# Four fused layers on one core: the first sequence's picked rows fetched as 32x32 tiles and turned by VectorE, and a new order of VectorE's work in the linear and the gated attention

## The chip, the core and the metric

The kernel runs on one core of one Trainium2 chip. A core has five engines with an instruction queue each: TensorE (PE in the profile; its weight loads are listed apart as PEld), VectorE (DVE), ScalarE (ACT), GpSimd (POOL) and SyncE (SP), which here issues nearly all transfers between the chip's memory (DRAM) and the core's working memory (SBUF). Matmuls write into eight accumulator banks (PSUM). The metric is the device time of one execution in microseconds (us), as a median of several runs.

## The reference

Two sequences of 1024 rows with 512 columns go through four layers. Each adds its result to its input and normalises every row.

```python
x = layernorm(x + linear_attention(x))     # 16 heads of 32
x = layernorm(x + fp4_ffn(x))              # 512 -> 2 x 1408 -> 512
x = layernorm(x + gated_attention(x))      # 16 heads, chunks of 64 rows
x = layernorm(x + expert_ffn(x))           # 512 of 1024 rows per sequence

# linear attention
q = elu(x @ Wq.T) + 1;  k = elu(x @ Wk.T) + 1;  v = x @ Wv.T
kv = einsum('bhtd,bhte->bhde', k, v)
z  = 1 / (einsum('bhtd,bhd->bht', q, k.sum(rows)) + 1e-6)
out = einsum('bhtd,bhde,bht->bhte', q, kv, z) @ Wo.T

# FP4 feed-forward: weights unpacked from 4-bit codes, one scale per 128 inputs
y = (silu(x @ w_gate.T) * (x @ w_up.T)) @ w_down.T
y = y / sqrt(mean(y * y) + 1e-6)

# gated attention
q = softmax(x @ Wq.T);  k = sigmoid(x @ Wk.T);  v = x
gf = log_sigmoid(-k)                 # decay, summed within a chunk of 64
o  = chunked_scan(q, k, v, gf)       # state S is carried from chunk to chunk
go = o @ Wog.T + x @ Wig.T
out = (o * rsqrt(mean(o * o) + 1e-5) * g_norm_w * silu(go)) @ Wo.T

# expert choice: the 512 rows with the highest score of each sequence
scores = x @ router_weight + router_bias
top, indices = top_k(scores, 512)
h = gelu(x[indices] @ w1 + b1)
out = zeros.at[indices].add((h @ w2 + b2) * sigmoid(top))
```

[...]

## The kernel before

The 2048 rows are held in SBUF in four blocks of 512 (two per sequence), `x_t[blk]`, each as four groups of 128 rows. Engines run their own queues in order; the order in a queue comes from a scheduler that follows the order of the program, and `tc.issue_after(ins)` tells it to place what follows behind a given instruction of the program. That is a hint of order, not a wait of its own. The feed-forward layer is ordered by hand.

**Seven products.** The large products (`by_seven`, `o_products`, `gate`, `hidden`) use a scheme with seven half-size products in place of eight: sums of input quarters are made first, products accumulate in a bank called `grow` and in side banks (`P2`, `P7`), and VectorE adds the results into place. A product's banks come from rings of banks (`rings["mm"]`, `rings["acc"]`), so a product can start only when VectorE or ScalarE has read what the bank held before.

**Linear attention** (lines 500 to 745). For each sequence b with blocks i = 2b and j = 2b + 1, the function `run(products, *others)` goes through the steps of one block's seven products and puts other work between them: `some_xk` (k times x, line 442), `turns` (PE turns weighed q rows, tile `qTp`, line 235), `some_o` (steps of `o_products`, the output products, whose results VectorE adds to x on line 571), `weigh` (lines 483 to 489: VectorE multiplies q with the sum of k, reduces it, takes the reciprocal and scales q), and `job(n)` (n steps of unpacking FP4 weights: a read of the packed codes `pk`, two VectorE steps on lines 288 and 289, one ScalarE step on line 292; `pk` has two buffers). In line 467 (`ksumb`) PE spreads the sum of k, which POOL adds up on lines 459 and 461. When a block's `o_products` are through, their last step takes the rows' statistics on VectorE (lines 226, 227, 218) and normalises the block on POOL: one power (line 219), four scalings of 128x512 (line 221). `split_quarter` (lines 264 to 268) turns the first block's rows for the next layer and splits them into a high part (ScalarE) and a low part `x1Tl` (VectorE, line 268).

**FP4 feed-forward** (lines 750 to 1300). Chunks of the hidden size pass through `gatep`, `upp` and `yp` products. `Normed.product` (line 1000) scales one row group's `yp` bank right after its product. At the end of the last chunk four groups are scaled; then the gated layer's first decayed keys follow (line 845, tile `rw`) and PE's first state updates (`up`, line 855).

**Gated attention** (loop over blocks from line 1875). `gate(blk)` is a generator: products `go`, with lines 1430 and 1431 multiplying a result into `uT`, later lines 1446 and 1449. `finish_by_seven` or `finish` (line 1515, tile `ao`) projects the result. Block 0 and block 1 are normalised for the router by `scored_rows` (line 221, and the score on line 1533, four each). `route` ranks the rows, and an indirect transfer by POOL (line 1579) scatters the picked rows into the DRAM table `picked`.

**Expert feed-forward.** `fetch` reads the picked rows back and turns them:

```python
nc.sync.dma_start(out=xs, in_=picked[b].rearrange("(c p) d -> p c d", p=P)[:, :, :C])
for i in range(4):
    pt = transposed(xs[:, i], "xsTp")
    nc.scalar.copy(room[:, :, i * P : (i + 1) * P], pt.rearrange("p (k t) -> p k t", k=KC))
```

`sums_of_x` (VectorE) makes their sums, `sums_of_w1` (VectorE, line 1980) those of the weights, `hidden` (line 1642, tile `hp`) multiplies them. `unpicked(blk)` takes statistics, normalises a block and writes it out (`out<-x`, line 1600), so that the rows that weren't picked have their result.

Of the kernel before, what the change touches and what calls it, by code (L numbers as in the profile page):

```python
# [21 lines left out]
P = 128  # L22
B, T, C = 2, 1024, 512
NB = 4
# [49 lines left out]
def body(ctx: ExitStack, tc: tile.TileContext, a: dict, out: bass.AP):  # L74
# [139 lines left out]
    def layernorm(x, mv, eps=1e-5, by=nc.vector):  # L214

        n = x.shape[1]
        rs = sp.tile([P, 4], F32, tag="rs", name="rs")
        nc.vector.tensor_scalar_add(rs[:, :n], mv[:, :, 1], eps)  # L218
        power = nc.gpsimd.tensor_tensor(rs[:, :n], rs[:, :n], const("mhalf")[:, :n], ALU.pow).ins  # L219
        for i in range(n):  # L220
            by.tensor_scalar(x[:, i], x[:, i], mv[:, i, 0:1], rs[:, i : i + 1], ALU.subtract, ALU.mult)  # L221
        return power
# [41 lines left out]
    def split_quarter(parts, blk, i, room=mm_bank):  # L264
# [3 lines left out]
        nc.vector.tensor_sub(lo, pt, hi.bitcast(F32))  # L268
# [111 lines left out]
    def by_seven(x, w, T, rooms, pairs, ready):  # L380
# [27 lines left out]
        nc.vector.tensor_add(c11, c11, p2)  # L408
# [69 lines left out]
    def weigh(blk, t):  # L478

        for r in range(2):  # L480
            x = pairs_of["q", blk][t][:, r]
            e = wk.tile([P, C], F32, tag="e", name="qk")
            nc.vector.tensor_mul(e, x, ksum_of[blk // 2])
            z = sp.tile([P, 16], F32, tag="z", name="z", bufs=2)
            nc.vector.tensor_reduce(z, e.rearrange("p (h d) -> p h d", d=32), AX.X, ALU.add)
            nc.vector.tensor_scalar_add(z, z, 1e-6)
            nc.vector.reciprocal(z, z)
            x3 = x.rearrange("p (h d) -> p h d", d=32)
            weighed[0] = nc.vector.tensor_mul(x3, x3, z.unsqueeze(2).to_broadcast([P, 16, 32])).ins

    weighed = [None]
# [61 lines left out]
    def o_products(blk):  # L553
# [6 lines left out]
        def product(ps, a, b, first, t, o):  # L560
# [10 lines left out]
            return nc.vector.tensor_add(x, x, ps.rearrange("p (r c) -> p r c", r=2)).ins  # L571
# [25 lines left out]
        yield  # L597
        mv = mv_of[blk] = sp.tile([P, 4, 2], F32, tag="mv", name="mv")
        with tc.issue_after(weighed[0]):
# [3 lines left out]
        yield  # L603
# [79 lines left out]
    def q_products(blk, ready):  # L683
        return by_seven(xT[blk], Wq, Ts["q"], S_rooms, pairs_of.setdefault(("q", blk), []), ready)
# [6 lines left out]
    for b in range(B):  # L691
        i, j = 2 * b, 2 * b + 1
        if b:
            run(
                k_products(i),
                turns(1, 0, 1) + job(1), job(1),
                turns(1, 2, 3) + some_o(1, 1) + job(1), some_o(1, 2) + job(1), some_o(1, 5) + job(1),
# [3 lines left out]
            k_products(j), [],  # L701
            some_xk(i, 0, 1) + job(2), some_xk(i, 2) + job(1) + q_ready, some_xk(i, 3) + job(1), job(1 + b),
# [3 lines left out]
        else:  # L706
# [7 lines left out]
            q_products(i, lambda t: weigh(i, t)), [],  # L714
            some_xk(j, 0, 1) + job(1 + b), some_xk(j, 2) + step(spread_ksum, b) + job(1), some_xk(j, 3) + job(1 + b),
        )
        if b == 0:
# [4 lines left out]
            q_products(j, lambda t: None),  # L722
# [4 lines left out]
            step(all_free) + some_o(i, 1) + step(weigh, j, 0) + split[3] + some_o(i, 3) + step(weigh, j, 1) + some_o(i, 1)  # L727
            + job(1 - b),
# [193 lines left out]
    with tc.tile_pool(name="s2", bufs=1) as wk2:  # L922
# [58 lines left out]
        class Normed:  # L981
# [8 lines left out]
            def product(self, i, g):  # L990
# [7 lines left out]
                if g == NI - 1 and i == 0:  # L998
                    self.y = place_w(3, "y")
                nc.vector.tensor_tensor(self.y[:, i] if g == NI - 1 else ps, ps, ratio[:, g], ALU.mult)  # L1000
# [174 lines left out]
        with tc.manual_schedule(engines={mybir.EngineType.PE, ACT, DVE, POOL}):  # L1175
# [38 lines left out]
            y_pair(LAST - 1, 1)  # L1214
            two = chunk_banks[1 - LAST % 2]
            free_banks = iter([*two, y_banks[3]])
            next_bank = lambda name: bank_tile(next(free_banks), name)
            gates.decayed(gates_at[3], gates_at[3], next_bank)
            new_spare(2)
            front(0, gates, gR["T2"][:, :, :P], next_bank)  # L1220
# [5 lines left out]
        rings["mm"] = (*chunk_banks[1 - LAST % 2], *y_banks[:2])  # L1226
        rings["acc"] = (*chunk_banks[LAST % 2], *y_banks[2:])
# [295 lines left out]
    def scored_rows(blk, mv=None):  # L1523

        if mv is None:
            mv = sp.tile([P, 4, 2], F32, tag="mv", name="mv")
            for i in range(4):
                row_stats(mv[:, i], x_t[blk][:, i])
        layernorm(x_t[blk], mv)
# [543 lines left out]
```

## Time and profile before

| What | us |
|---|---|
| Median of 3 runs | 896.24 (895.79 to 896.49) |
| The profiled execution's own time | 895.37 |
| Its span | 893.6 |
| PE busy within the span | 879.2 (98%) |
| DVE busy | 686.7 (77%) |
| ACT busy | 379.0 (42%) |
| POOL busy | 261.3 (29%) |

The granted TensorE clock is 0.997 over the span. Busy shares are an average over four layers with different limits. All times below are measured from the span's start. In the feed-forward layer, from 240 to 480 us, PE is busy 239.82 of 240 us; DVE is busy 49.08 of the 50 us from 85 to 135, and 57.76 of the 66 us from 605 to 671.

A line of the trace's time views gives the start, the time to the end of the last instruction of a group, the engine, the line of the program, the operation and its tiles, the number of instructions, and in brackets the idle time of that engine before it with what ended that idle time. In the list of waits the three numbers are the sum, the count and the longest.

### The profile page before, as it was taken

The numbers are of one execution on the slowest core, as the hardware profiler recorded it, in microseconds if no ns is written. First come the engines' busy times: TensorE is split into PE (matmuls) and PEld (weight loads), VectorE is DVE, ScalarE is ACT, GpSimd is POOL, SyncE is SP. The second block draws the span as 40 slices with busy tenths as digits, with TensorE's granted clock in tenths as the row PEclk, the third lists the DMA queues.
The fourth block names the chain that finished last, engine by engine and source line by source line (L and its number), as shares of the span: only waits on it lengthen the run. The fifth ranks groups of instructions, "written<-read, shape, count | busy, mean of one in ns | idle before, by whom it ended". The sixth has DMA issues, their size and how long they took to land. (4 is left out here: it accounts for less than half of the span.)

```text
span 893.6 us, 10909 instructions
## 1 busy us (share of the span) xinstructions
PE 879.2 (98%) x3923; PEld 687.5 (77%) x3923; DVE 686.7 (77%) x1320; ACT 379.0 (42%) x648; POOL 261.3 (29%) x229
## 2 busy tenths in 40 slices
PE   9999999999999999999999999999999999999996
PEld 6668876688678888888876787788586888888886
DVE  3569995589787787887779986848976976998535
ACT  2345342463477797887867333221202223210000
POOL 2020075200474358556655320020340030000112
PEclk9999999999999999999999999999999999999998
DMA  9632221211421503414102344000034220320001
GB/s 327 222 98 80 73 68 48 74 45 19 97 110 48 47 1 86 57 55 111 25 25 73 69 114 169 1 1 1 6 106 141 78 95 1 133 104 1 12 36 48
DMA packets 88007, 64.85 MB, mean 73 GB/s; under 512 B 63214, under 2 KB 63770, under 8 KB 87441
## 3 DMA queue, kind: packets, MB, share of 16 engines
q1 hardware_dynamic: 85313, 58.89, 22.9%
q0 software_dynamic: 1920, 4.22, 1.2%
q10 hardware_dynamic: 720, 1.05, 0.4%
q8 instruction: 31, 0.51, 0.2%
q14 instruction: 23, 0.19, 0.1%
HBM read 48.37 MB, written 17.88 MB: 74 GB/s over the span
## 5 line engine op out<-in xcount | busy, mean ns | idle before, releaser
L1000 DVE TENSOR_TENSOR yp<-yp,ratio 128x512 f32<-128x512 f32 x160 | 103.3, 693 | 17.2 <-PE yp L941 16.7
L219 POOL TENSOR_TENSOR rs<-rs,table 128x4 f32<-128x4 f32 (+1 forms) x19 | 17.2, 906 | 299.2 <-DVE rs L218 298.9
L966 ACT ACTIVATE gatep<-gatep,scale 128x512 f32<-128x512 f32 x132 | 83.9, 659 | 35.8 <-PE gatep L941 26.5
L941 PE MATMUL gatep<-x1Th,wgu 128*128 128x512 f32 x176 | 70.2, 399 | 0.0
L941 PE MATMUL yp<-wdn,hhi 128*128 128x512 f32 x176 | 70.1, 398 | 0.0
L941 PE MATMUL yp<-wdn,hlo 128*128 128x512 f32 x176 | 69.9, 397 | 0.2 <-POOL hlo L975 0.2
L941 PE MATMUL gatep<-x1Tl,wgu 128*128 128x512 f32 x176 | 69.3, 394 | 0.3 <-DVE x1Tl L268 0.3
L941 PE MATMUL upp<-x1Tl,wgu 128*128 128x512 f32 x176 | 68.8, 391 | 0.0
L941 PE MATMUL upp<-x1Th,wgu 128*128 128x512 f32 x176 | 68.8, 391 | 0.0
L966 ACT ACTIVATE upp<-upp,scale 128x512 f32<-128x512 f32 x100 | 64.9, 664 | 6.7 <-PE upp L941 3.7
L975 POOL TENSOR_TENSOR hlo<-whole,hhi 128x512 fp32r<-128x512 f32 x43 | 55.6, 1292 | 3.5
L974 POOL CAST hhi<-whole 128x512 fp32r<-128x512 f32 x43 | 26.3, 612 | 88.4 <-DVE whole L972 86.9
L972 DVE SCALAR_TENSOR_TENSOR whole<-upp,scale,silu 128x512 f32<-128x512 f32 x43 | 32.3, 750 | 19.8 <-PE upp L941 11.5
L909 PE MATMUL go<-spare,spare 128*128 128x256 f32 x192 | 44.5, 382 | 0.0
L442 PE MATMUL xk<-pair,x 128*128 128x512 f32 x96 | 42.7, 592 | 0.0
L226 DVE BATCH_NORM_STATS2 st<-x 128x6 f32<-128x512 f32 x64 | 42.3, 678 | 0.4
L909 PEld LDWEIGHTS go<-spare,spare 128*128 128x128 f32 x192 | 35.8, 190 | 7.4 <-issue 2.8
L941 PEld LDWEIGHTS yp<-wdn,hhi 128*128 128x128 f32 x176 | 33.1, 188 | 9.5 <-DVE yp L1000 1.0
L941 PEld LDWEIGHTS gatep<-x1Th,wgu 128*128 128x128 f32 x176 | 33.0, 188 | 9.2 <-ACT gatep L966 1.1
L941 PEld LDWEIGHTS gatep<-x1Tl,wgu 128*128 128x128 f32 x176 | 33.1, 188 | 8.2 <-DVE x1Tl L268 0.6
L941 PEld LDWEIGHTS yp<-wdn,hlo 128*128 128x128 f32 x176 | 33.1, 188 | 8.0 <-POOL hlo L975 0.6
L941 PEld LDWEIGHTS upp<-x1Th,wgu 128*128 128x128 f32 x176 | 33.1, 188 | 7.3 <-DVE rw L972 0.2
(469 smaller groups left out, 2067.8 us busy)
## 6 DMA issues: line engine op xcount, KB each, us to landing
pk<-in_gu SPq DMA_DIRECT2D x16, 352.0 KB, 3.7
x<-in_x SPq DMA_DIRECT2D x4, 1024.0 KB, 14.9
w<-in_w SPq DMA_DIRECT2D x1, 4096.0 KB, 12.3
xs<-picked SPq DMA_DIRECT2D x4, 1024.0 KB, 4.9
out<-x SPq DMA_DIRECT2D x4, 1024.0 KB, 4.5
w<-in_w SPq DMA_DIRECT2D x4, 1024.0 KB, 7.4
x0T<-in_xT SPq DMA_DIRECT2D x3, 1024.0 KB, 7.3
x1r<-x SPq DMA_DIRECT2D x3, 1024.0 KB, 5.1
```

The lines of the kernel that those rows point to most:

```text
L219: power = nc.gpsimd.tensor_tensor(rs[:, :n], rs[:, :n], const("mhalf")[:, :n], ALU.pow).ins
L226: nc.vector.bn_stats(st, x)
L442: ins = nc.tensor.matmul(acc_of[b][c], x_t[blk][:, i, c * P : (c + 1) * P], pairs_of["k", blk][i // 2][:, i % 2], start=blk % 2 == 0 and i ...
L909: ins = nc.tensor.matmul(ps[:, 256 * m : 256 * m + 256], w[:, k, m], b[:, k, 256 * half : 256 * half + 256], start=first and m == 0 and k ...
L941: nc.tensor.matmul(ps, w, x, start=start and n == 0, stop=stop and n == 1, skip_group_check=True)
L966: nc.scalar.activation(ps, ps, AF.Copy, scale=s)
L972: nc.vector.scalar_tensor_tensor(self.whole, ps, s, self.silu, ALU.mult, ALU.mult)
L974: nc.gpsimd.tensor_copy(hi, self.whole)
L975: nc.gpsimd.tensor_sub(lo, self.whole, hi.bitcast(F32))
L1000: nc.vector.tensor_tensor(self.y[:, i] if g == NI - 1 else ps, ps, ratio[:, g], ALU.mult)
```

## The change

Four places change.

1. **Linear attention.** The statistics and the normalisation leave `o_products` and become `norm(blk)`. In the second sequence's schedule block 0 is normalised within the k products of block 3, block 1 within the q products of block 2, and block 2 at the very end behind the weighing of block 3. Several VectorE steps are ordered behind others: the weighing of odd blocks behind additions of the output products, the `x1Tl` subtractions and one addition of `by_seven` behind the weighing. PE's turning of rows for block 1 moves behind the second product (`P<-Wk`). Unpacking steps are distributed differently, 27 in all as before.
2. **End of the FP4 feed-forward.** For the last two row groups of the last chunk the scaling is parted from the product: products, then the decayed keys, then the scalings. The banks that the first state updates use, and the two rings behind them, are exchanged accordingly.
3. **Gated attention.** `scored_rows` and `unpicked` are parted into statistics with the root (`root_of_rows`), which stay where they were, and the scaling with what follows it, which moves behind steps of the gate. Both treat the rows of block 0: they are scored in block 1's turn of the loop, now behind that turn's last gate addition, and normalised for the output in block 3's turn, now behind line 1431. The sums of w1 are ordered behind that line too.
4. **First sequence's picked rows.** One read of 1 MB, 16 PE transposes and 4 ScalarE copies are replaced by 16 reads of 64 KB (32 partitions, each 16 runs of 128 bytes) and 4 VectorE transposes of 32x32 tiles over 128x512. The reads are issued by SP when block 3's turn in the loop begins. The second sequence's `fetch` is as before.

```diff
+    def root(mv, eps=1e-5):
...
         nc.vector.tensor_scalar_add(rs[:, :n], mv[:, :, 1], eps)
+        nc.gpsimd.tensor_tensor(rs[:, :n], rs[:, :n], const("mhalf")[:, :n], ALU.pow)
+        return mv, rs
+
+    def to_norm(x, mv, rs, by=nc.vector):
+        for i in range(x.shape[1]):
             by.tensor_scalar(x[:, i], x[:, i], mv[:, i, 0:1], rs[:, i : i + 1], ALU.subtract, ALU.mult)
...
         nc.scalar.copy(hi, pt)
-        nc.vector.tensor_sub(lo, pt, hi.bitcast(F32))
+        with tc.issue_after(weighed[0]):
+            nc.vector.tensor_sub(lo, pt, hi.bitcast(F32))
...
         p2 = product(mm_bank("P2"), A12, B21, True)
-        nc.vector.tensor_add(c11, c11, p2)
+        with tc.issue_after(behind_add) if behind_add else contextlib.nullcontext():
+            nc.vector.tensor_add(c11, c11, p2)
...
+            with tc.issue_after(adds[-2 + r]) if blk % 2 else contextlib.nullcontext():
+                nc.vector.tensor_mul(e, x, ksum_of[blk // 2])
...
-            return nc.vector.tensor_add(x, x, ps.rearrange("p (r c) -> p r c", r=2)).ins
+            adds.append(nc.vector.tensor_add(x, x, ps.rearrange("p (r c) -> p r c", r=2)).ins)
+            return adds[-1]
...
+    def norm(blk):
+
         mv = mv_of[blk] = sp.tile([P, 4, 2], F32, tag="mv", name="mv")
-        with tc.issue_after(weighed[0]):
+        with tc.issue_after(anchor[0] if blk < 2 else weighed[0]):
             for i in range(4):
                 row_stats(mv[:, i], x_t[blk][:, i])
             layernorm(x_t[blk], mv, by=nc.gpsimd)
-        yield
...
-                turns(1, 0, 1) + job(1), job(1),
-                turns(1, 2, 3) + some_o(1, 1) + job(1), some_o(1, 2) + job(1), some_o(1, 5) + job(1),
+                [], turns(1, 0, 1),
+                turns(1, 2, 3) + some_o(1, 1), some_o(1, 2), some_o(1, 4) + [lambda: anchor.__setitem__(0, adds[-1])] + job(1),
...
-            k_products(j), [],
-            some_xk(i, 0, 1) + job(2), some_xk(i, 2) + job(1) + q_ready, some_xk(i, 3) + job(1), job(1 + b),
+            k_products(j), job(b),
+            some_xk(i, 0, 1) + job(2), some_xk(i, 2) + job(1 + b) + q_ready,
+            some_xk(i, 3) + (step(norm, 0) if b else []) + job(1 + b), job(1 + b),
...
-            q_products(i, lambda t: weigh(i, t)), [],
-            some_xk(j, 0, 1) + job(1 + b), some_xk(j, 2) + step(spread_ksum, b) + job(1), some_xk(j, 3) + job(1 + b),
+            q_products(i, lambda t: weigh(i, t)), job(b),
+            some_xk(j, 0, 1) + (step(norm, 1) if b else []) + job(1 + b), some_xk(j, 2) + step(spread_ksum, b) + job(1), some_xk(j, 3) + job(1 + b),
...
-            step(all_free) + some_o(i, 1) + step(weigh, j, 0) + split[3] + some_o(i, 3) + step(weigh, j, 1) + some_o(i, 1)
-            + job(1 - b),
+            step(all_free) + some_o(i, 1) + split[3] + some_o(i, 1) + step(weigh, j, 0) + some_o(i, 2) + step(weigh, j, 1)
+            + (step(norm, i) if b else []) + job(1 - b),
...
+                if scaled:
+                    self.scale(i, g)
+
+            def scale(self, i, g):
+
+                ps = self.ps[i]
                 nc.vector.tensor_tensor(self.y[:, i] if g == NI - 1 else ps, ps, ratio[:, g], ALU.mult)
...
-            y_pair(LAST - 1, 1)
+            for i in (2, 3):
+                normed[NB - 1].product(i, NI - 1, False)
             two = chunk_banks[1 - LAST % 2]
-            free_banks = iter([*two, y_banks[3]])
+            free_banks = iter([*two, y_banks[1]])
             next_bank = lambda name: bank_tile(next(free_banks), name)
             gates.decayed(gates_at[3], gates_at[3], next_bank)
             new_spare(2)
+            for i in (2, 3):
+                normed[NB - 1].scale(i, NI - 1)
             front(0, gates, gR["T2"][:, :, :P], next_bank)
...
-        rings["mm"] = (*chunk_banks[1 - LAST % 2], *y_banks[:2])
-        rings["acc"] = (*chunk_banks[LAST % 2], *y_banks[2:])
+        rings["mm"] = (*chunk_banks[1 - LAST % 2], y_banks[0], y_banks[3])
+        rings["acc"] = (*chunk_banks[LAST % 2], y_banks[2], y_banks[1])
...
+    def scored_rows(blk, mv=None, rooted=None):
+
+        to_norm(x_t[blk], *(rooted or (root(mv) if mv is not None else root_of_rows(blk))))
...
+    def unpicked(blk, rooted=None):
+
+        to_norm(x_t[blk], *(rooted or root_of_rows(blk, 0.25e-5)))
...
             with tc.issue_after(scored_next):
-                scored_rows(0)
+                rooted = root_of_rows(0)
...
         if blk == 3:
+            xsS = xT_tile("xs")
+            for g in range(4):
+                for k in range(KC):
+                    at = P * k + 32 * g
+                    nc.sync.dma_start(
+                        out=xsS[32 * g : 32 * g + 32, k].rearrange("j (tr i) -> j tr i", i=32),
+                        in_=picked[0][:, at : at + 32].rearrange("(tr j) i -> j tr i", j=32),
+                    )
             with tc.issue_after(scored):
-                unpicked(0)
+                rooted = root_of_rows(0, 0.25e-5)
...
+            if n == 3 and blk == 1:
+                with tc.issue_after(done):
+                    scored_rows(0, None, rooted)
+            if n == 1 and blk == 3:
+                with tc.issue_after(done):
+                    unpicked(0, rooted)
+                p7_added = done
...
-    sums_of_w1((0,))
-    _, xs = fetch(0)
+    xs = xT_tile("xsT")
+    with tc.issue_after(p7_added):
+        sums_of_w1((0,))
+        for i in range(4):
+            nc.vector.transpose(xs[:, :, tile_of(i)], xsS[:, :, tile_of(i)])
     xs = sums_of_x(xs, W1oT)
     finish(3)
-    sums_of_w1((1,))
+    with tc.issue_after(p7_added):
+        sums_of_w1((1,))
```

## The prediction

> **What bounds the kernel now.** I read the busy times first, then the waits of PE, then the chain, then the time views of VectorE, POOL and SP around each wait.
>
> ```profile
> span 893.6 us, 10909 instructions
> PE 879.2 (98%) x3923; PEld 687.5 (77%) x3923; DVE 686.7 (77%) x1320; ACT 379.0 (42%) x648; POOL 261.3 (29%) x229
> ```
>
> PE is idle for 893.6 − 879.2 = 14.4 us, of which the start takes 1.04 and the tail behind PE's last product (886.25) 7.35. So the change can win only PE work that it takes away and what is left of PE's waits.
>
> ```profile
> PE go L909 <- DVE uT L1431: 2.2, 2, 1.9
> PE grow L565 <- DVE x L571: 1.5, 2, 0.8
> PE up L855 <- DVE rw L845: 0.8, 1, 0.8
> PE grow L565 <- DVE qS L520: 0.6, 1, 0.6
> PE P L565 <- DVE x L571: 0.4, 1, 0.4
> PE gatep L941 <- DVE x1Tl L268: 0.3, 1, 0.3
> ```
>
> Each of these ends with a VectorE instruction in a stretch where VectorE is full (49.08 of 50 us busy from 85 to 135, 57.76 of 66 from 605 to 671). PE waits because of the order of VectorE's queue. The chain shows the PE work in question:
>
> ```profile
> 670.67 3.72 PE go L909 x16
> 674.39 1.75 PE xsTp L235 x16
> 676.13 13.74 PE ao L1515 x32
> 689.87 10.36 PE hp L1642 x48
> ```
>
> PE's own queue loses those 16 transposes and otherwise only changes places. So a wait that goes moves everything behind it forward, as long as nothing else comes late.
>
> **1. Linear attention.** Waits of 0.40 (99.85), 0.68 (102.53), 0.55 (118.91) and 0.82 (130.36). The first two: x<-P on line 571 starts at 99.12, because line 347 ahead of it waits for ScalarE's `e` until 98.51; its product was done at 97.73. Now it stands ahead of lines 483 and 485, so it runs at 97.75 and x<-grow near 99.7: both waits go. The turning of block 1's rows now stands behind `P<-Wk` (near 106.7), and the weighed rows end at 103.5 and 105.6, so no new wait there. The third and fourth are late VectorE queues, with eight statistics and POOL's normalisation in the same stretch:
>
> ```profile
> 115.97 10.41 POOL L221 TENSOR_SCALAR x<-x,mv,rs 128x512 f32<-128x512 f32 x4
> 228.45 8.26 POOL L221 TENSOR_SCALAR x<-x,mv,rs 128x512 f32<-128x512 f32 x4
> ```
>
> Beside the first, line 519 took 1.09, line 288 1.01 and line 347 1.75 us, against 0.5 to 0.69 elsewhere. With statistics and normalisation gone, line 520 is ready near 113.8 (PE wants it at 117.3) and line 571 reads near 126 (PE 127.9). Gain 0.40 + 0.68 + 0.55 + 0.82 = 2.45.
>
> Where it goes: VectorE is busy 12.98 of 26 us from 135 to 161 and 16.09 of 25 from 161 to 186, so its time there costs nothing. POOL is the question. Block 1's normalisation now stands ahead of the last four sums of k, which `ksumb` waits for. Before, these sums ended at 165.0 and PE read them at 175.21; after, PE reads at 175.21 − 2.45 = 172.76. The statistics end near 155.9 (the last pair's elu at 152.2, then 3.5 us of statistics and a `pk` step). Then one power (1.01 to 2.04), four scalings (8.26 to 10.54) and four sums (2.62 + 2.78 = 5.4; 5.1 to 5.7) end between 170.5 and 174.4: 2.2 us early to 1.6 late. The nearest execution of the same scalings stands at 138.95, with a power of 1.05 and 10.54; that gives 155.9 + 1.05 + 10.54 + 5.4 = 172.9, and I take 0.2 as lost.
>
> The Trainium skill, "SBUF — State Buffer", section "SBUF: two separate sides", says that VectorE and GpSimd lock a shared port pair for a whole instruction and the other blocks fully. The trace bears it out in part: VectorE's steps did grow beside the scalings, but the scalings took 10.41 us beside a full VectorE (10.40 of 10.40 busy), 10.54 beside one that was half idle (5.39 of 10.6), and 8.26 beside another (4.95 of 8.4). By the rule a VectorE busy 16.09 of 25 us leaves POOL between these, below 10.4, and the 0.2 falls away; by the nearest row it stays. The unpacking steps (27 as before) only move. Their reads land in 3.7 us on two buffers, and the longest wait of VectorE for one was 3.29 (145.29), in the half idle stretch. In front of the k products of the next pair VectorE has 1.8 us left; a read 1.8 us later than that would cost.
>
> End of the layer: the fourth `x1Tl` is ready near 211.0 for 215, so 0.30 (216.64) goes. Weighing block 3 moves later: its first half is ready at 216.13 for PE's 216.17, its second at 218.18 for 217.52. I take 0.5 lost (0 to 0.7). Block 2's normalisation (POOL until 236.71) is used by transfers needed at 256.3, 20 us of cover. Sum of the part: 2.45 + 0.30 − 0.2 − 0.5 = 2.05.
>
> **2. End of the FP4 layer.** `up` waits 0.75 for line 845 at 489.48, which stands behind four scalings (487.09, 2.48). With two of them behind it, its input (ScalarE, 487.80) decides and it ends near 488.7; PE's transposes before `up` end near 489.1. Gain 0.75, with about 0.4 us in hand. The two delayed scalings move the normalisation's inputs by 1.2 us; VectorE is continuous from 494.7 to 512, but at 494.70 it waits 1.49 us for PE, which absorbs them.
>
> **3. Gated attention.** Waits of 0.25 (574.07) and 1.91 (670.67), both for line 1431.
>
> ```profile
> 664.64 0.16 DVE L218 TENSOR_SCALAR rs<-mv 128x4 f32<-128x4 f32 x1
> ...
> 666.30 1.92 DVE L221 TENSOR_SCALAR x<-x,mv,rs 128x512 f32<-128x512 f32 x4 [0.90 <-POOL rs L219]
> ...
> 669.93 0.68 DVE L1431 TENSOR_TENSOR uT<-uT,go 128x512 f32<-128x512 f32 x1
> ```
>
> Here line 1431 stands behind a normalisation that waits for POOL's power, and a sum of w1. With them behind it, it runs when its product is there: about 570.4 in block 1's turn, 662.2 to 662.8 in block 3's, where the `go` products run through to 669.0. Both waits go: 2.16. Moved behind: in block 1's turn 1.82 + 4 × 0.61 = 4.28 us, so the `uT` sums end at 585.9 in place of 581.93; PE reads them at 592.18, and VectorE stands idle 4.29 ahead of 586.21. In block 3's turn the `uT` pairs end at 669.0 and 671.15 for `ao` at 669.05 and 672.5. Without that cover up to 1.5 us comes back.
>
> **4. Picked rows.** PE's 16 transposes go, from 674.23 to 675.97: 1.74 (ScalarE's copies go with them, ScalarE being idle there). Added: 16 reads and 4 VectorE transposes. The same transposes stand in the trace:
>
> ```profile
> 530.78 2.49 DVE L1247 STREAM_TRANSPOSE x2T<-x2S 128x512 f32<-128x512 f32 x4 [0.98 <-DMA x2S<-x2r]
> ```
>
> SP's queue:
>
> ```profile
> 360.69 6.67 SPq L255 DMA_DIRECT2D x2S<-x2r  x8
> ...
> 423.76 8.14 SPq L255 DMA_DIRECT2D x2S<-x2r  x8
> ...
> 657.63 0.37 SPq L1606 DMA_DIRECT2D xs<-picked  x1
> ```
>
> and the list of transfers (KB each, median us from issue to landing):
>
> ```profile
> x2S<-x2r SPq DMA_DIRECT2D x32, 64.0 KB, 2.4
> ```
>
> The read starts when the scatter has landed, after the earlier gains (2.05 + 0.75 + 0.25) near 657.63 − 3.1 = 654.5. Reads of 64 KB in the same 128-byte runs leave SP every 0.65 to 1.07 us (6.67 and 8.14 for eight: 0.83 and 1.02) and land in 2.4. The last of 16 lands between 654.5 + 15 × 0.65 + 2.4 = 666.7 and 654.5 + 15 × 1.07 + 2.4 = 673.0, the transposes end by 675.5. The first `hp` wants them at 689.71 − 3.1 − 1.9 − 1.7 = 683.0, and its first two products need no sums, which VectorE makes beside them. So 7 us of cover at the least. In SP's queue the output of block 0 and four w2 loads stand behind the reads, 10 to 17 us later; w2 was loaded by 690.82 and is needed at 789. Gain 1.74.
>
> The Trainium skill, "DMA: Bandwidth & Descriptors", speaks against this part: "Specifications" asks for 512 bytes for line rate, and "Anatomy of one DMA" gives each transfer a fixed cost of about 2.0 us. Paid 16 times in series, that estimate is 32 us, the last read lands at 686.5, and the time would be about 895.5. The trace's spacing shows reads in such runs overlapping, which speaks for the sum as it stands.
>
> **Sum.** 2.05 + 0.75 + 2.16 + 1.74 = 6.70. The profiled execution took 895.37 (its span 893.6 and 1.77 around it) and stands 0.87 below the median: 888.67 for such an execution, 896.24 − 6.70 = 889.5 on the median. The forecast's own range is 888.6 (the 0.7 of losses in part 1 don't come, and 0.2 of scatter) to 890.5 (1 us of B's loss).
>
> **Rivals.**
>
> *B. POOL takes back part of the linear attention's gain.* The sums of k come at 174.4, 1.6 late where I took 0.2, and weighing costs 0.7: 889.5 + 1.4 + 0.2 = 891.1. For it: scalings of 10.41 and 10.54 and a power of 2.04 stand in the trace. Against: the one of 8.26.
>
> *C. The gated wait stays.* If another VectorE step keeps line 1431 back as before, or the `uT` pairs come late by as much, 2.16 isn't won: 891.7. For it: VectorE is busy 57.76 of 66 us there. Against: the new order has line 1431 directly behind its product.
>
> *D. The 16 reads land late and the kernel gets slower.* A last landing later than 683.0 − 2.5 = 680.5 costs; the kernel is slower than before when `hp` starts after 689.71, so from a landing at 687.2, which a spacing of (687.2 − 654.5 − 2.4) / 15 = 2.0 us gives. Reads wholly in series, 16 × 2.4 = 38.4, land at 692.9; `hp` starts at 695.4, 12.4 late: 901.9. For it: these reads gather rows just scattered. Against: the spacing of 0.83 to 1.02. (The page's fixed cost, above, is this rival's mechanism.)
>
> *E. The gain isn't passed on.* A transfer or VectorE takes PE's place as the bound further down: 893 to 896. Against: from 676 to the tail PE's waits are 0.05 in all, and the second sequence's read is issued by a step that moves along.
>
> **How the numbers follow.** Chances: forecast 0.60, B 0.17, C 0.08, E 0.06, D 0.09. The range reaches from 887.8 (nothing lost, 888.8, and 1.0 below it, the size of one wait that I may have left standing elsewhere) over B and C to 893.2, the lower end of E; E's rest and D, 0.14, are left out. No change here means within 0.2%, about 1.8 us and what a measurement can tell: faster is under 894.45. The forecast, B, C and a third of E are faster, 0.87; two thirds of E same, 0.04; D slower, 0.09.
>
> **What would show it.** Part 1: no waits on lines 571, 520 and 268 in PE's list, and none for POOL's `ksum`; a wait there is B. Part 2: none for `rw`. Part 3: none for line 1431, which starts within 0.1 us of its product's end. Part 4: no `xsTp` in the first sequence, 16 reads under 1.1 us apart, `hp` directly behind `ao`. A PE wait for `xs` or its sums there makes the prediction wrong and D right; a new wait of over 3 us anywhere else, or `hp` starting at 683 with the end not moving along (E), does the same for the sum.

## The result and the profile after

The changed kernel takes 890.77 us (median of 4 runs, 890.62 to 890.97), the kernel before 896.33 (4 runs, 895.79 to 896.49). The ratio is 0.9939, with a 95% interval of 0.9924 to 0.9955. So it is 5.6 us faster, where 6.7 was forecast (889.5). The time lies in the forecast's range, 0.3 us from rival B's 891.1. The profiled execution took 890.63, its span 888.8.

These are the busy times of the changed kernel and, from the list of PE's waits, those of 0.4 us and more (the sum, the count, the longest):

```profile
span 888.8 us, 10912 instructions
...
PE 877.1 (99%) x3907; PEld 686.0 (77%) x3907; DVE 686.9 (77%) x1324; ACT 376.6 (42%) x644; POOL 257.1 (29%) x229
```

```profile
PE idle L365 <- DVE ones L361: 1.0, 1, 1.0
PE grow L397 <- ACT pair L425: 0.8, 1, 0.8
PE kp L647 <- DMA Wk<-in_WkT: 0.6, 1, 0.6
PE x1Tp L240 <- DVE x1Tl L274: 0.5, 1, 0.5
PE xsTp L240 <- DMA xs<-picked: 0.4, 1, 0.4
PE vk L509 <- DVE pair L433: 0.4, 1, 0.4
PE qTp L240 <- DVE pair L497: 0.4, 1, 0.4
```

Every wait that the prediction wanted gone is gone: none on the output products' additions (line 571 before, 579 now), none on `qS`, `rw` or `uT`, and the one on the first `gatep` too. In their place stand four in the linear attention, between 179 and 221: 0.81, 0.40, 0.54 and 0.39. The 0.4 on `xsTp` belongs to the second sequence's read. The 0.6 on `Wk` is the load of the first weights at the start; it is missing or smaller in the other traces with the same beginning, so it isn't the change's.

PE's queue at the place of part 4 and the chain from there:

```profile
660.52 3.62 PE L921 MATMUL go<-x2T,Wig 128*128 128x256 f32 x16
663.98 3.62 PE L921 MATMUL go<-spare,spare 128*128 128x256 f32 x16
667.43 3.62 PE L921 MATMUL go<-spare,Wog 128*128 128x256 f32 x16
670.88 13.90 PE L1536 MATMUL ao<-W1o,uT 128*128 128x512 f32 x32
684.62 3.62 PE L1661 MATMUL hp<-xsT,w 128*128 128x256 f32 x16
```

The `go` products run into `ao` and `ao` into `hp` without a gap, and `xsTp` is gone. `hp` starts at 684.62, 5.09 us ahead of the 689.71 before. How the reads and the transposes came about, in SP's and in VectorE's queue:

```profile
656.45 8.31 SPq L1969 DMA_DIRECT2D xs<-picked  x16
```

```profile
664.25 0.69 DVE L1452 TENSOR_TENSOR uT<-uT,go 128x512 f32<-128x512 f32 x1 [1.14 <-PE go L921]
664.85 1.91 DVE L224 TENSOR_SCALAR x<-x,mv,rs 128x512 f32<-128x512 f32 x4
...
673.55 2.48 DVE L2021 STREAM_TRANSPOSE xsT<-xs 128x512 f32<-128x512 f32 x4
```

Line 1452 (1431 before) now waits for its product and not behind a normalisation. The reads leave every 0.52 us and land in 2.4, so the last is there near 667. The transposes wait for nothing; they stand in VectorE's queue until 673.55 and are done 8.6 us before `hp`.

A table of four PE positions shows where the gain was made and where it was lost (start in us):

| PE instruction | before | changed | difference |
|---|---|---|---|
| `ksumb`, linear attention | 175.21 | 172.10 | −3.11 |
| first `yp` with a wait, FP4 layer | 246.20 | 246.33 | +0.13 |
| first `hp` | 689.71 | 684.62 | −5.09 |
| second sequence's `xsTp` | 737.42 | 732.68 | −4.74 |

The linear attention was 3.11 us ahead at 172 (3.45 in the kernel with part 1 alone) and had lost all of it when the next layer began. The loads at the start of the kernel shift whole traces against each other: the first sequence's `ksumb`, ahead of everything that the change moves, stands at 61.75 before and at 62.15 in the changed kernel (61.81 with part 1 alone). Counted from there the lead at 172 is 3.51 in both kernels.

### The profile page after: what moved, and what is told of

Same layout as the page of the kernel before. It is cut to its first block, busy times and chain, and to the rows that moved or that the text cites. A ratio compares the mean times of both kernels' runs of the same rounds, so it can differ in the third digit from the quotient of the medians.

```text
span 888.8 us, 10912 instructions
## 1 busy us (share of the span) xinstructions
PE 877.1 (99%) x3907; PEld 686.0 (77%) x3907; DVE 686.9 (77%) x1324; ACT 376.6 (42%) x644; POOL 257.1 (29%) x229
## 4 chain that ended last, share of the span: by engine, by line
PE 79%; issue 7%; DVE 7%; DMA 3%; POOL 2%; ACT 1%; POOLq 0%; SPq 0%; DVEq 0%; ACTq 0%
PE yp L1750 10%; PE yp L953 9%; PE gatep L953 9%; PE upp L953 9%; PE go L921 8%; PE hp L1661 6%; PE xk L449 5%; PE grow L397 4%; PE P L397 3%; PE grow L573 2%; PE P L573 2%; PE grow L1500 2%; PE ao L621 2%; PE kp L647 2%; PE op L1361 1%
```

## The experiments

### Which part brings what

`no_part1` undoes part 1 and keeps the others. `part1_alone` and `part4_alone` add one part to the kernel before. In `part4_alone` the transposes stand where the kernel before had its `fetch`:

```diff
-    _, xs = fetch(0)
+    xs = xT_tile("xsT")
+    for i in range(4):
+        nc.vector.transpose(xs[:, :, tile_of(i)], xsS[:, :, tile_of(i)])
```

> The changed kernel without its part 1 (linear attention as before; parts 2 to 4 kept). Theory T1: part 1 won its four waits and the x1Tl wait (2.75 us) but made new ones of 0.81 (179.10, behind ScalarE's unpacking step), 0.40 (184.94), 0.54 (196.76) and 0.39 (220.65), so it is worth only about 0.6 us: this kernel takes 5.0 us less than before, about 891.4, and the four new waits are gone from PE's list while the five old ones (0.40, 0.68, 0.55, 0.82, 0.30) are back. Rival T2: part 1 is worth its predicted 2.05 and the missing microsecond lies in the other parts: this kernel takes 3.5 us less than before, about 892.8.

> The kernel before with part 1 alone. T1: 0.6 us less than before, about 895.7, with the new waits of 0.81, 0.40, 0.54 and 0.39 at the places where the changed kernel has them. T2: 2.05 less, about 894.3, with no such waits.

> The kernel before with the tile reads and VectorE's transposes of part 4 alone. Prediction: 1.74 us less than before, about 894.6, if PE's work alone counts. Rival: the second sequence's read, which PE met with a wait of 0.05 before and of 0.40 in the changed kernel, doesn't follow PE wholly, since VectorE's ranking ahead of it has four transposes more in its queue: 1.4 less, about 894.9, with a wait of about 0.4 at the second xsTp.

| Kernel | us (median) | ratio to before, 95% interval |
|---|---|---|
| without part 1 | 890.65 | 0.9934 (0.9918 to 0.9951) |
| part 1 alone | 895.94 | 0.9994 (0.9984 to 1.0005) |
| part 4 alone | 894.35 | 0.9977 (0.9965 to 0.9988) |

The kernel before took 896.13 beside them. Without part 1 the kernel is 5.5 us faster than before, as fast as the whole change; part 1 alone can't be told from nothing. So T2 falls: the interval of part 1 alone ends at a gain of 1.4 us, below 2.05. Whether it is worth T1's 0.6 or nothing the times don't tell; the traces say 0.1 to 0.3 (last column of the table below). As T1 expected, the kernel without part 1 has the five old waits back and none of the four new ones. Part 4 alone brings 1.8 (1.1 to 3.1 by the interval), its predicted 1.74, with a wait of 0.19 at the second `xsTp`. Parts 2 and 3 were not run apart. PE's waits in `part1_alone`:

```profile
178.96 1.99 PE L397 MATMUL grow<-Wq,rw 128*128 128x256 f32 x8 [1.02 <-ACT pair L425]
184.81 3.84 PE L509 MATMUL vk<-G,Wv 128*128 128x128 f32 x32 [0.40 <-DVE pair L433]
196.62 0.66 PE L240 MATMUL x1Tp<-table,x 128*128 128x128 f32 x4 [0.54 <-DVE x1Tl L274]
...
220.51 0.63 PE L240 MATMUL qTp<-table,pair 128*128 128x128 f32 x4 [0.39 <-DVE pair L497]
246.20 0.51 PE L953 MATMUL yp<-wdn,hlo 128*128 128x512 f32 x1 [0.18 <-POOL hlo L987]
```

The last line starts at 246.20, as before, though `ksumb` was 3.45 us earlier (171.76). (That the hundredth agrees is luck: with the linear attention as it was, it starts at 246.25 in `no_part1` and at 246.59 in `part4_alone`.) That is the mark of a second chain with a time of its own. The first four waits add up to 2.35; of the rest, 0.79 went where PE counts as busy but is paced (`gp` was 1.37 long before and is 2.16 now).

### The second chain

VectorE's queue from 185 to 197, in the kernel before and in part 1 alone, is the weighing of block 2's q (lines 483 to 489, 492 to 497 after). Its first multiplication starts at 186.28 before and at 186.38 in part 1 alone. From 186 to 197 VectorE is busy 10.86 of 11 us in both. In the kernel before PE came to this point without a wait, so the chain shows nowhere in PE's list; it is as long as PE's own work there. What starts it, though, is not the same in the two. In the kernel before, VectorE's additions wait for PE's product, and the exponential `e` is ready only 0.17 ahead of the line that uses it (its end, 184.69 + 0.63, against 185.49):

```profile
184.88 0.69 DVE L426 TENSOR_TENSOR pair<-pair,P 128x512 f32<-128x512 f32 x1 [0.96 <-PE P L391]
185.49 0.68 DVE L347 SCALAR_TENSOR_TENSOR pair<-grow,e 128x512 f32<-128x512 f32 x1
186.28 1.29 DVE L483 TENSOR_TENSOR qk<-pair,ksum 128x512 f32<-128x512 f32 x2
```

In part 1 alone PE's product comes earlier and the exponential does not:

```profile
184.07 0.68 DVE L433 TENSOR_TENSOR pair<-pair,P 128x512 f32<-128x512 f32 x1
185.58 0.69 DVE L353 SCALAR_TENSOR_TENSOR pair<-grow,e 128x512 f32<-128x512 f32 x1 [0.83 <-ACT e L352]
186.38 1.29 DVE L492 TENSOR_TENSOR qk<-pair,ksum 128x512 f32<-128x512 f32 x2
```

What holds it back is ScalarE's queue, here in the changed kernel:

```profile
183.39 1.15 ACT L298 ACTIVATE wdn<-pk 128x512 fp32r<-128x512 f16 x2 [1.41 <-DVE pk L295]
184.45 0.58 ACT L351 ACTIVATE e<-grow 128x512 f32<-128x512 f32 x1
185.06 0.63 ACT L352 ACTIVATE e<-e 128x512 f32<-128x512 f32 x1
```

The weighing needs that exponential `e`, and it stands behind two unpacking steps which wait for VectorE. The same three lines stand in the trace before, at 183.03, 184.08 and 184.69. Ahead of them another unpacking step waits for its read, and the copy that PE needs stands behind it; this is the 0.81. VectorE's queue shows the read:

```profile
176.05 0.91 DVE L294 TENSOR_SCALAR pk<-pk,shift 128x512 int32<-128x512 int32 x1 [2.07 <-DMA pk<-in_dn]
176.99 0.43 DVE L295 TENSOR_SCALAR pk<-pk 128x512 int32<-128x512 int32 x1
```

The next runs take this apart. `job_earlier` moves one unpacking step out of that stage, `jobs_4_9_3` three:

```diff
# job_earlier
-            q_products(i, lambda t: weigh(i, t)), job(b),
+            q_products(i, lambda t: weigh(i, t)), [],
...
-                turns(1, 2, 3) + some_o(1, 1), some_o(1, 2), some_o(1, 4) + [lambda: anchor.__setitem__(0, adds[-1])] + job(1),
+                turns(1, 2, 3) + some_o(1, 1), some_o(1, 2), some_o(1, 4) + [lambda: anchor.__setitem__(0, adds[-1])] + job(2),
# jobs_4_9_3
-            q_products(i, lambda t: weigh(i, t)), job(b),
+            q_products(i, lambda t: weigh(i, t)), [],
...
-            some_xk(j, 0, 1) + (step(norm, 1) if b else []) + job(1 + b), some_xk(j, 2) + step(spread_ksum, b) + job(1), some_xk(j, 3) + job(1 + b),
+            some_xk(j, 0, 1) + (step(norm, 1) if b else []) + job(1 + b), some_xk(j, 2) + step(spread_ksum, b) + job(1), some_xk(j, 3) + job(1 - b),
...
-                turns(1, 2, 3) + some_o(1, 1), some_o(1, 2), some_o(1, 4) + [lambda: anchor.__setitem__(0, adds[-1])] + job(1),
+                turns(1, 2, 3) + some_o(1, 1), some_o(1, 2) + job(1), some_o(1, 4) + [lambda: anchor.__setitem__(0, adds[-1])] + job(3),
```

> The changed kernel with one unpacking step moved from the first place of block 2's q products to the last place of block 2's k products (the steps by stage 2, 9, 5 in place of 1, 9, 6). Theory: the 0.81 at 179.10 and the 0.40 at 184.94 come from the chain of pk reads: a read issued late lands at 175.95, VectorE's two steps and ScalarE's step follow, and ScalarE's copies for PE stand behind that step. With one step less in that stage both waits go and nothing comes back: 1.2 us less than the changed kernel, 6.7 us less than before. Rival: POOL's scalings and sums slow VectorE's steps there (1.40, 1.50 and 1.37 us in place of 0.47), and with the slow steps still there the wait stays within 0.3 us of 1.2, or the step moved into the full stretch before 135 brings a wait of its own: no less than 0.2 from the changed kernel.

> The changed kernel with three unpacking steps moved from block 2's q products (6 there, now 3: the one at the first place and the two at the last) to block 2's k products (1 there, now 4). Theory: from 185.5 to 197.5 VectorE runs without a gap in the kernel before and with part 1 alone, at the same times to 0.1 us (185.49 and 185.58 for line 347/353), though PE came there 3.45 us earlier. That stretch of VectorE is the bound of the layer's end, and it starts late because ScalarE's exponentials for the first of the two weighings stand behind two unpacking steps (183.39 to 184.45) and, before, behind the one that waits for its read. With these steps gone from there VectorE's stretch starts about 2 to 3 us earlier: the waits of 0.81 and 0.40 go and those of 0.54 and of the G products (gp busy 2.16 in place of 1.37) shrink: 2 us less than the changed kernel, 7.5 less than before, about 888.7. Rival: the stretch is set by PE's products or by the sum of k, and only the 1.2 us of the two first waits come, as in the run with one step moved (0.5 less): no less than 889.6. Against both: the stretch before 135 is full and gets waits on line 571 back.

`job_earlier` took 890.25 (ratio 0.9929, 0.9913 to 0.9946). The 0.81 went, but a wait of 0.29 came on another `grow` and 0.28 stayed at `vk`: a gain of half a microsecond by the medians (the intervals overlap), not 1.2. The theory of the reads holds for the place and is wrong on the size. `jobs_4_9_3` took 889.34 (0.9912, 0.9893 to 0.9930), between the two expectations; the weighing began 1.2 us earlier, where 2 to 3 were expected. Three of the four new waits are gone (the 0.4 on `qTp` stays), and there are two that no expectation had:

```profile
173.80 1.12 PE L474 MATMUL ksumb<-ksum,ones 128*128 128x512 f32 x2 [1.22 <-POOL ksum L468]
175.22 1.99 PE L397 MATMUL grow<-Tq 128*128 128x256 f32 x8 [0.30 <-ACT pair L419]
```

This is the prediction's rival B at last: POOL normalises block 0 (158.55, 9.68 us) ahead of the last four sums of k (168.19, 5.56 us). The opposite order was the next test, with the changed kernel's unpacking (`sums_first_only`), with 4, 9 and 3 steps (`sums_first`) and with 5, 9 and 2 (`sums_first_5`). The cut shows `sums_first` against `jobs_4_9_3`; `norm` now calls its two parts one after the other:

```diff
+    def norm_stats(blk):
+        mv = mv_of[blk] = sp.tile([P, 4, 2], F32, tag="mv", name="mv")
+        with tc.issue_after(anchor[0] if blk < 2 else weighed[0]):
+            for i in range(4):
+                row_stats(mv[:, i], x_t[blk][:, i])
+
+    def norm_rows(blk):
+        with tc.issue_after(anchor[0] if blk < 2 else weighed[0]):
+            layernorm(x_t[blk], mv_of[blk], by=nc.gpsimd)
...
-            some_xk(i, 3) + (step(norm, 0) if b else []) + job(1 + b), job(1 + b),
+            some_xk(i, 3) + (step(norm_stats, 0) if b else []) + job(1 + b), job(1 + b),
...
-            q_products(i, lambda t: weigh(i, t)), [],
+            q_products(i, lambda t: weigh(i, t)), step(norm_rows, 0) if b else [],
```

> The changed kernel with POOL's power and scalings of block 0 issued behind the last four sums of k in place of ahead of them (statistics and unpacking steps as in the changed kernel). If POOL's queue is what keeps the linear attention's gain back (the sums end at 171.57 where PE wants them at 172.10, and POOL's sums slow VectorE's unpacking steps to 1.4 us): the waits of 0.81 and 0.40 go, 1.2 us less than the changed kernel. If the chain of pk reads does it, the read at 172 to 176 is still late and both waits stay: within 0.4 of the changed kernel.

> The kernel with three unpacking steps moved (4, 9 and 3 by stage), and POOL's scalings of block 0 behind the sums of k. With the steps moved, POOL's sums became late (ksumb waited 1.22 at 173.80, which the changed kernel did not show). Theory: each of the two covers the other; with both undone the wait on ksumb and the 0.30 behind it go, and PE reaches VectorE's stretch of weighing with little lost: 1.0 us less than with the steps alone, 8.3 less than before, about 888.0. Rival: VectorE's stretch from 185 begins no earlier, since a pk read (1.36 late at 176.60) and ScalarE's copies behind it still set it: less than 0.4 from the kernel with the steps alone.

> As the run before, with one more unpacking step moved from block 2's q products to block 2's k products (5, 9 and 2 by stage), so that no read of codes falls between 172 and 177. Theory of the reads: 0.5 to 1 us less than with 4, 9 and 3, about 887.3, with PE's waits from 170 to 200 under 0.5 in sum. Rival: no change, or a wait on line 571/579 before 135, where VectorE gets fuller.

| Kernel | us (median) | ratio to before | `ksumb` (PE) | weighing starts (DVE) | first `yp` with a wait (PE) | weighing to `yp` | first sequence's `ksumb` to `yp` |
|---|---|---|---|---|---|---|---|
| before | 896.33 | | 175.21 | 186.28 | 246.20 | 59.92 | 184.45 |
| changed | 890.77 | 0.9939 | 172.10 | 186.51 | 246.33 | 59.82 | 184.18 |
| `part1_alone` | 895.94 | 0.9994 | 171.76 | 186.38 | 246.20 | 59.82 | 184.39 |
| `job_earlier` | 890.25 | 0.9929 | 172.02 | 185.88 | 245.69 | 59.81 | 183.64 |
| `jobs_4_9_3` | 889.34 | 0.9912 | 173.80 | 185.32 | 245.39 | 60.07 | 182.93 |
| `sums_first_only` | 890.71 | 0.9945 | 172.02 | 186.93 | 246.75 | 59.82 | 184.68 |
| `sums_first` | 888.08 | 0.9910 (0.9895 to 0.9926) | 171.78 | 183.79 | 243.74 | 59.95 | 181.91 |
| `sums_first_5` | 888.87 | 0.9914 | 172.72 | 183.97 | 244.46 | 60.49 | 181.69 |

The last two columns carry the argument. The next layer starts 59.8 to 60.1 us after the weighing's first multiplication in all of these kernels but the last, wherever PE was at `ksumb`: PE's position at 172 moved by up to 3.45 us and didn't matter, the weighing's start did. The last column leaves out what the start of a trace adds by chance. By it, POOL's order alone (`sums_first_only`) gains nothing, since the reads still hold ScalarE; the steps alone bring 1.25 us over the changed kernel and then meet POOL; the order on top of them brings 1.02 more, as its theory expected. In device time, both together bring 2.6 us over `sums_first_only`, measured on the same chip. That the order adds to the steps rests on the traces, for by their ratios `jobs_4_9_3` and `sums_first` can't be told apart. `sums_first` has the lowest median of all, 888.08 where 888.0 was expected. The trace shows its weighing right behind its exponential:

```profile
181.56 0.69 DVE L405 TENSOR_TENSOR rw<-Tq,x0T 128x512 f32<-128x512 f32 x1
182.59 0.69 DVE L353 SCALAR_TENSOR_TENSOR pair<-grow,e 128x512 f32<-128x512 f32 x1 [0.34 <-ACT e L352]
183.20 0.68 DVE L433 TENSOR_TENSOR pair<-pair,P 128x512 f32<-128x512 f32 x1
183.79 1.28 DVE L492 TENSOR_TENSOR qk<-pair,ksum 128x512 f32<-128x512 f32 x2
```

The fifth step moved brought little: the read is gone, but now the exponential waits 1.14 us for PE's product, and the weighing starts where it did. Of the expected half microsecond the last column shows 0.2. Its median lies 0.8 above `sums_first` (its runs from 887.41 to 889.29). In the profiled execution that is the start alone: PE is 0.94 late at the first sequence's `ksumb`, ahead of everything in which the two kernels differ. For its other runs nothing on record gives a reason.

### An order that looked guilty

The change puts one addition of block 3's q products behind the weighing. In part 1 alone ScalarE's exponential waits for it (until 196.00) and the copies of the turned rows stand behind that. `c11_free` takes the order out:

```diff
-            q_products(j, lambda t: None, weighed[0] if b else None),
+            q_products(j, lambda t: None),
```

> The changed kernel without the order that puts one addition (c11, P2) of block 3's q products behind the weighing. Rival theory: that order costs the 0.8 us at the G products, since ScalarE's exponential waits for the addition (196.00) and the copies of the turned rows stand behind it (197.20): with it undone, 0.8 less than the changed kernel. Theory of the full VectorE: the addition then stands ahead of the second row's weighing, which ends 1.3 us later, and the second qTp waits instead: within 0.3 of the changed kernel.

It took 890.45 (0.9926, 0.9907 to 0.9944), and its `yp` starts at 246.29 where the changed kernel has 246.33 (184.56 after the first `ksumb`, where that has 184.18). The waits only changed hands: 0.65 on the second `qTp` and 0.64 on `x1Tp` in place of 0.54 on `x1Tp` and the slow `gp`. Turning round two members of a full chain didn't shorten it.

### The cover of the reads

`reads_x4` issues the 16 reads four times over, to the same place. `second_tiles` fetches the second sequence's rows in the same way as the first's:

```diff
# reads_x4
-            for g in range(4):
+            for g in (*range(4), *range(4), *range(4), *range(4)):
# second_tiles
-        later.extend(fetch(1, room))
-        return last_turned[0]
+        xs1 = xT_tile("xs")
+        for g in range(4):
+            for k in range(KC):
+                at = P * k + 32 * g
+                nc.sync.dma_start(
+                    out=xs1[32 * g : 32 * g + 32, k].rearrange("j (tr i) -> j tr i", i=32),
+                    in_=picked[1][:, at : at + 32].rearrange("(tr j) i -> j tr i", j=32),
+                )
+        later.extend((xs1, room))
+        return last_hp[0]
...
     def next_sums():
+        for i in range(4):
+            nc.vector.transpose(room[:, :, tile_of(i)], later[0][:, :, tile_of(i)])
```

> The changed kernel with the second sequence's picked rows fetched in the same way, 16 reads and VectorE's transposes in place of one read and 16 PE transposes. There the read has no cover: PE already waits 0.40 for it. PE's 1.77 and that wait go; the 16th read leaves SP 15 x 0.52 us after 727.4 and lands 2.4 later, at 737.6, the transposes end at 740.1, where the first hp product of that sequence stood at 736.18: 3.9 us more than the changed kernel, a wait of about 6 us on the transposed rows. Rival: if the gain of part 4 were PE's work in itself, 2.2 us less.

> The changed kernel with the 16 reads of the first sequence issued four times over (the same rows to the same place). A test of the cover of part 4. If the reads leave SP every 0.52 us as in the changed kernel, the last of 64 lands at 656.45 + 63 x 0.52 + 2.4 = 691.6, the transposes end at 694.1, and hp starts 9.5 us later than its 684.62: about 9.5 to 10 us more than the changed kernel. If part 4 had cover only by PE's ao products and VectorE's queue behind the transposes counted too, more than 12. If the reads don't matter, no change.

`reads_x4` took 902.05 (1.0052, 1.0032 to 1.0072), 11.3 more than the changed kernel by the medians (10.1 by the ratios). `second_tiles` took 895.94 (0.9988, 0.9978 to 0.9998), 5.2 more (4.4 by the ratios), where 3.9 was expected. Both show the wait that was expected, and in the profiled executions both cost more than it. PE's waits, the one of `reads_x4` first:

```profile
694.51 6.46 PE L1661 MATMUL hp<-xsT,w 128*128 128x256 f32 x16 [9.19 <-DVE xsT L2021]
```

```profile
739.42 6.53 PE L1661 MATMUL hp<-row,w 128*128 128x256 f32 x16 [5.49 <-DVE row L2058]
```

In `second_tiles`, a wait of 5.49 less the 2.17 that this kernel saves (16 transposes, 1.77, and the 0.40) is 3.3. But the first 16 products behind the wait take 6.53 us where 3.62 is their time elsewhere: 2.9 more, and 3.3 + 2.9 = 6.2 is the difference of the two profiled executions (896.78 and 890.63). In `reads_x4`, `hp` starts 9.9 us later than in the changed kernel, about as expected, and its first 16 products take 6.46, 2.8 more; 12.7 is again the difference of the profiled executions (903.35 and 890.63). The last section tells why.

So rival D's mechanism is real, and it was a matter of place: with 8.6 us of cover the reads are free, at a read that PE is waiting for they cost 4 to 5 us.

## Why the prediction was right and wrong

**The sign, the range and three parts were right.** Parts 2 to 4 were priced at 0.75 + 2.16 + 1.74 = 4.65. The kernel without part 1 is 5.5 faster than before by medians, and its profiled execution 5.1 (895.37 to 890.30), with a wait of 0.27 at the second sequence's read.

They brought more than their price because a wait that goes frees more than the list says. The `go` products around the longest wait, before:

```profile
665.14 3.62 PE L909 MATMUL go<-spare,spare 128*128 128x256 f32 x16
670.67 3.72 PE L909 MATMUL go<-spare,Wog 128*128 128x256 f32 x16 [1.91 <-DVE uT L1431]
```

They start 5.53 apart; in the changed kernel it is 3.45 (663.98 and 667.43). That is 2.08, and the products behind the wait took 3.72 in place of 3.62: 2.18 for a listed 1.91. The four waits of part 1 show the same, 2.45 listed and 3.51 freed at `ksumb`. So most waits in the sum were about 0.26 too small (the 0.75 of `up`, from `tp` to `up` 1.02 before and 0.21 after, by less).

That the time lies in the range is in part luck: two errors went against each other, part 1's 2.05 that hardly came and 0.4 to 0.8 that the other parts brought beyond their price.

- *Part 2.* The keys' multiplication ended at 488.92 (forecast 488.7), `up` followed the transposes at 489.36 without a wait, as forecast.
- *Part 3.* Both waits went, and nothing came back: 31.00 of 31 us busy from 640 to 671, before 29.09.
- *Part 4.* Its 1.74 was measured alone as 1.8. The reads were issued at 656.45, not 654.5, because part 1's gain wasn't there; the spacing was 0.52, below the lower end of 0.65. The sum needed none of it, the cover was larger than either. The section of the Trainium skill that the prediction cites for the fixed cost of 2.0 us describes transfers that GpSimd issues, and these left SyncE's queue; reads of 2.4 us that leave every 0.52 us paid nothing in series.

**Part 1 was wrong: 2.05 forecast, 0 to 0.2 measured by the medians.** Its first half was right. All four waits went, and PE reached `ksumb` 3.1 us earlier (3.45 in part 1 alone). The step that failed is the sentence on the way there: "So a wait that goes moves everything behind it forward, as long as nothing else comes late", with the unpacking steps set at nothing because they "only move". I looked for what would be late among PE's releasers one by one, and for VectorE's time by shares: 16.09 of 25 us busy from 161 to 186 "costs nothing". The share was right and the conclusion wrong. In that half idle stretch ScalarE's queue held an exponential behind unpacking steps, these behind VectorE's, these behind a read, and the weighing that all waited for began at 186.28 before and at 186.51 after. The shares also stopped at 186, where VectorE's full stretch begins: 10.86 of the next 11 us. (That each of the six waits listed stands where VectorE is full was read too widely as well: those at 217, 489 and 574 lie outside the two stretches given.) One unpacking step more in that stage (6 in place of 5) cost about half a microsecond, as `job_earlier` shows; what the steps of 1.4 us beside POOL's sums cost, where 0.47 is normal, no run shows by itself. This is rival E's mechanism, another engine taking PE's place as the bound, at a place where E did not look for it.

**Rival B's time came, not its mechanism.** The sums of k ended at 171.57, 0.53 before PE asked; POOL cost nothing in the changed kernel, where 0.2 was taken as lost. (The prediction named the normalisation ahead of them block 1's; it is block 0's. And its own terms put the end of the sums between 170.3 and 174.2, not 170.5 and 174.4.) POOL came to bind only when the unpacking was out of the way, in `jobs_4_9_3`, with 1.22 us. The weighing of block 3 cost 0.39 (forecast 0.5). The `x1Tl` wait of 0.30 went, and another of 0.54 at an earlier `x1Tp` belongs to the second chain.

**The lock.** The Trainium skill, "SBUF — State Buffer", section "SBUF: two separate sides", gives a rule and no price; with it the prediction put POOL's scalings below 10.4 in the new place, and by the nearest row at 10.5. They took 9.34 beside a VectorE busy 6.92 of the 9.34 and, for the next block, 8.58 beside one busy 4.83 of 8.57. So the estimate by the rule was nearer here. But the rows follow no order of VectorE's share (10.43 where it was busy 8.46 of 10.43 in `sums_first`, 8.25 where it was busy 6.39 of 8.25 in `sums_first_5`, 10.54 at 5.39 of 10.54 before), so the rule isn't shown. The page limits the lock to VectorE instructions in a two-port mode or with two inputs in SBUF; the prediction left that out.

**E in small.** The second sequence's read made PE wait 0.40, before 0.05. In the other kernels it was 0.18 to 0.70 without an order that follows PE's position; `sums_first`, 2.7 us ahead there, has 0.27. I take it for the scatter of a landing time that PE meets within half a microsecond; no run separates it.

## What to carry to other kernels

A wait in the list of the bounding engine is worth its time only up to the next chain that is as long. Before a saving is moved down the trace, look for a stretch where the second engine runs without a gap, and ask what starts it: if its start hangs on something that the change doesn't move, the gain ends there. Small steps with a wait of their own (here the unpacking of weights behind a read) belong where no one queues behind them, in ScalarE's queue too. And a bundle should be measured part by part: here three parts made the whole gain, and the fourth, rearranged, gave as much again as half of theirs.

## What the runs showed of the hardware

A long idle of PE cost more than its length. These are stretches of `second_tiles` around its wait: the stretch and its length, the busy times of PE, PEld, VectorE, ScalarE and POOL with their instructions, the granted TensorE clock, the share of the DMA engines and GB/s.

```profile
730.00:734.00 4.00, 3.94 (x19) 3.12 (x17) 2.00 (x4) 1.03 (x2) 0.00 (x0) 1.00 0.87 124
734.00:739.40 5.40, 0.00 (x0) 0.01 (x1) 2.09 (x4) 1.64 (x3) 0.00 (x0) 0.90 0.52 67
739.40:743.00 3.60, 3.58 (x9) 2.89 (x10) 3.53 (x6) 0.00 (x0) 0.00 (x0) 0.50 0.00 0
743.00:746.00 3.00, 3.00 (x10) 2.46 (x9) 0.12 (x1) 0.59 (x1) 0.00 (x0) 0.64 0.00 0
746.00:750.00 4.00, 4.00 (x20) 3.53 (x19) 1.93 (x3) 0.00 (x0) 0.00 (x0) 1.00 0.01 4
```

After 5.4 us without a product PE works at half its clock for nearly 6 us (3.6 at 0.50, and about 2.2 of the next 3.0, since 0.64 is their mean), which adds 2.9 us. `reads_x4` shows the same behind its 9.2: 0.50 and 0.65, then 1.00. Behind the wait of 1.91 in the kernel before the clock was 1.00. The Trainium skill, "TensorE: Matmul & The Clock Gate", section "What's actually happening", gives half the clock after an idle window of about 3.4 us and full clock after a busy one; the halves agree, the way back took nearly 6 us here. Rival D had left this out: here a read so late that PE stood still for five microseconds cost three more.

VectorE beside POOL, beyond the prediction: an unpacking step on VectorE (128x512) that takes 0.43 to 0.49 us alone took 1.37 to 1.50 in the changed kernel beside POOL's sums of k (166.14 to 171.57). Beside POOL's scalings it took 0.49 (165.22) and 0.91 (176.05).
